# Layer 3's band matrices kept by pairs of outputs instead of tiles by outputs

## The chip, the cores and the metric

The kernel runs on one core of a Trainium2 chip. The metric is the device time of one execution in microseconds (us). Three runs of the kernel before gave 8943.62, 8946.06 and 8962.98 us; the median, 8946.06 us, is the time before. The profile is of a further execution, of 8976.86 us.

## The reference

A network of four layers works on x, 16 images of 64 x 64 pixels with 256 channels, in float32. Each layer is a residual block on the group-normalised input:

```
x = x + L0(gn(x))   # linear attention over the 4096 pixels, 8 heads
x = x + L1(gn(x))   # gated channels, a state-space scan over the pixels, batch norm
x = x + L2(gn(x))   # involution, 3 x 3 kernels made from the pixel itself
x = x + L3(gn(x))   # involution, 7 x 7 kernels made from the pixel itself
```

Only layer 3 is touched. It computes, with G = 16 groups of 16 channels:

```
r    = relu(bn(x @ w_reduce))                  # 256 -> 64
kgen = (r @ w_span + b_span).reshape(B, H, W, 16, 49)
out[b, h, w, g, c] = sum over the 49 taps k of kgen[b, h, w, g, k] * patch[b, h, w, k, g, c]
```

Every pixel has its own 49 weights for each group, and the 16 channels of a group share them.

## The kernel before

The layers run one after the other. Layer 3 is the last section of the program and takes the stretch from about 6608 us to the end.

**Tiles.** The image is cut into tiles of TR x TC = 3 x 8 output pixels: 22 rows of 8 tiles, so NTL = 176 tiles of TILE_OUT = 24 outputs. The input of a tile is 9 x 14 = 126 pixels (TILE_IN), which lie on the partitions. For a tile and a group, the 7 x 7 involution of the 24 outputs is one matrix product: a band matrix of 126 input pixels by 24 outputs, against the 126 pixels by the channels. The band matrix holds kgen at the 49 places of a column where the tap is, and zero elsewhere.

**The band matrices** are made by `matrices(i, quarter)` (L1362) for image i and a quarter of the channels, which is 4 groups. A quarter has two buffers `w` (tag "wm", pool of four buffers, so that of two quarters one is read while the other is made), one for each pair of groups: 128 partitions, and for each of them 176 tiles x 48 outputs (two groups of 24) of float32. Each buffer is made in 12 steps n of four output columns:

- TensorE (L1380): four float32 matmuls, each 64 rows (`span`, a shifted copy of the span weights) by 176 columns (`rt`, r for all 176 tiles at one output place). The profile records each float32 matmul as two instructions, each with its weight load. The results go to one of three PSUM tiles `pk` (tag "wg"), as [2, 2, 176]: b and m number the four outputs, and the last axis is the tile.
- The step's 4 x 176 numbers go from PSUM to `w` with the bias `spanb` added. In 14 of a quarter's 24 steps VectorE does it in one instruction of 704 elements (L1395); in the other 10 ScalarE does it in four of 176 elements (L1390). The innermost axis of each is the tile t, whose numbers are one after the other in PSUM and 48 floats (192 bytes) apart in `w`.

**The involution** is `involution7` (L1437), one turn for image i, a quarter, and t of NTT = 11. A turn has two rows of tiles (k = 0, 1), 8 tiles each, and two pairs of groups q: 32 float32 matmuls (L1446) of 126 rows, 32 output channels (`xw`, the patches, as weights) and 48 moving columns, the tile's slice of `w[q]`, 48 floats in a row. The four matmuls of one tj have their results on four different quarters of the partitions of the PSUM tile `pa`. ScalarE (L1456) and VectorE (L1457) then combine the two groups of a pair with masks into `ex`, and GpSimd (L1464) adds the residual `rx`.

**Order.** The loop at L1488 has 704 turns (16 images x 4 quarters x 11). A turn issues on SyncE's queue the patches of four turns ahead (L1414), the residual (L1434), the stores of finished outputs (L1526) and now and then the next image's features (L1314). Then come `involution7`, and `STEPS[t]` (3, 2, 2, 3, ...) steps of `matrices` for the quarter that is to come, so that 24 steps fit into 11 turns, and in many turns `reduced` (L1347 and L1354), which makes `rt` of the next image. The first quarter's matrices are made before the loop. In this section the order of the text is not binding: the framework's planner orders each engine's instructions by the place in the text and by when it reckons that operands and buffers are free, and places the semaphores. The order is fixed when the kernel is built.

`reduced` (L1347) has matmuls whose moving operand is read in pairs of floats, every second pair of a row (`"p (x b v) -> p b x v"`, b = 2, v = 2): the first pass of the chip over a layout like that of the change.

Of the kernel before, what the change touches and what calls it, by code (L numbers as in the profile page):

```python
# [9 lines left out]
F32 = mybir.dt.float32  # L10
# [5 lines left out]
P = 128  # L16
# [12 lines left out]
TR, TC = 3, 8  # L29
NTR, NTC = 22, HW // TC  # L30
TILE_IN = (TR + 6) * (TC + 6)
TILE_OUT = TR * TC
# [4 lines left out]
def network(ctx: ExitStack, tc: tile.TileContext, a: dict, out: bass.AP):  # L37
# [139 lines left out]
    with ExitStack() as st:  # L177
# [399 lines left out]
        for n in range(LAST + 16):  # L577
            m, t = divmod(n, NCH)
# [64 lines left out]
    with ExitStack() as st:  # L643
# [24 lines left out]
        with tc.tile_pool(name="s_conv", bufs=1) as pcv:  # L668
# [8 lines left out]
            for dj in range(7):  # L677
                dst = band if dj == 0 else term
# [22 lines left out]
        for n in range(10):  # L701
            delta, c = n // 2, n % 2
# [3 lines left out]
                rhs=maps[:, c, :, delta : delta + NB],  # L706
# [5 lines left out]
        m = maps[:, 0, :, 2 : 2 + NB]  # L712
# [18 lines left out]
        with tc.manual_schedule():  # L731
# [25 lines left out]
            for n, (ch, g) in enumerate(steps):  # L757
# [18 lines left out]
                b, k = g * 8, min(8, NI - g * 8)  # L776
# [8 lines left out]
        n = NI * NCH  # L785
# [500 lines left out]
    with ExitStack() as st:  # L1286
        pc = st.enter_context(tc.tile_pool(name="c_const", bufs=1))
        wk = st.enter_context(tc.tile_pool(name="c_work", bufs=2))
        wm_p = st.enter_context(tc.tile_pool(name="c_wm", bufs=4))
# [70 lines left out]
        NTL = NTR * NTC  # L1360

        def matrices(i, quarter):  # L1362


            rto = rts[i % 2].rearrange("k a b t u -> k (a b) (t u)")
            wms[i, quarter] = wm = []
            for q in range(2):
                w = wm_p.tile([P, NTL, 2 * TILE_OUT], F32, tag="wm", name="wm")
                wm.append(w)
                first = quarter * 4 + q * 2  # L1370
                for n in range(12):

                    pk = wg.tile([P, 2, CT], F32, tag="wg", name="pk")
                    pkv = pk[:, :, 0 : 2 * NTL].rearrange("p b (m t) -> p b m t", m=2)
                    for m in range(2):
                        for b in range(2):
                            gg, o = divmod(n * 4 + b * 2 + m, TILE_OUT)
                            s0 = SPAN - P - (o // TC * (TC + 6) + o % TC)
                            half = slice(b * 64, b * 64 + 64)
                            nc.tensor.matmul(  # L1380
                                pkv[:, b, m],
                                lhsT=span[half, first + gg, s0 : s0 + P],
                                rhs=rto[half, o // 4 * 2 + m, :],
                                start=True, stop=True,
                            )
                    g0 = first * TILE_OUT + n * 4
                    dst = w[:, :, n * 4 : n * 4 + 4].rearrange("p t (b m) -> p b m t", b=2)
                    if (q * 12 + n) % 12 in (1, 3, 6, 8, 11):
                        for m in range(4):
                            nc.scalar.activation(  # L1390
                                dst[:, m // 2, m % 2], pkv[:, m // 2, m % 2], AF.Identity,
                                bias=spanb[:, g0 + m : g0 + m + 1],
                            )
                    else:
                        nc.vector.tensor_tensor(  # L1395
                            dst, pkv,
                            spanb[:, g0 : g0 + 4].rearrange("p (b m) -> p b m", b=2).unsqueeze(
                                3
                            ).broadcast_to([P, 2, 2, NTL]),
                            ALU.add,  # L1400
                        )
                    yield
# [3 lines left out]
        NTT = NTR // 2  # L1406
# [30 lines left out]
        def involution7(i, quarter, t, wm, msk, xw, ex, rx):  # L1437


            pa = sm.tile([P, CT], F32, tag="sm", name="pa")  # L1440
            pav = pa[:, 0 : 2 * TR * HW].rearrange("c (g a w) -> c (g a) w", g=2, w=HW)
            for tj in range(NTC):
                for k in range(2):
                    for q in range(2):
                        p0 = 64 * k + 32 * q
                        nc.tensor.matmul(  # L1446
                            pav[p0 : p0 + 32, :, tj * TC : (tj + 1) * TC],
                            lhsT=xw[0:TILE_IN, k, tj, 32 * q : 32 * q + 32],
                            rhs=wm[q][0:TILE_IN, (t + k * NTT) * NTC + tj, :].rearrange(
                                "p (g w) -> p g w", w=TC  # L1450
                            ),
                            start=True, stop=True,
                        )
            pag = pa[:, 0 : 2 * TR * HW].rearrange("c (g t) -> c g t", g=2)
            h, pr = divmod(quarter, 2)
            nc.scalar.activation(ex, pag[:, 0], AF.Identity, scale=msk[:, pr, h, 0:1])  # L1456
            nc.vector.scalar_tensor_tensor(  # L1457
                ex, pag[:, 1], msk[:, pr, h, 1:2], ex, ALU.mult, ALU.add
            )
            parts = [(slice(0, P), TR * HW)]  # L1460
            if t == NTT - 1:
                parts = [(slice(0, 64), TR * HW), (slice(64, P), HW)]
            for p, m in parts:
                nc.gpsimd.tensor_tensor(ex[p, 0:m], ex[p, 0:m], rx[p, 0:m], ALU.add)  # L1464
# [19 lines left out]
        for _ in matrices(0, 0):  # L1484
            pass
        done = []
        gap = min(44, (4 * NTT * (NI - 1) - 4) // NCH)
        for n, (i, quarter, t) in enumerate(turns):  # L1488
# [17 lines left out]
            if t == 0:  # L1506
                making = iter(())
                if n + NTT < len(turns):
                    making = matrices(*turns[n + NTT][:2])
# [17 lines left out]
            if n + 2 in features:  # L1527
                cs[features[n + 2]] = load_reduced(*features[n + 2])
            involution7(i, quarter, t, wms[i, quarter], msk, pats.pop(0), ex[:, t % 2], rx[:, t % 2])
            if n % gap == 2 and n // gap < NCH:  # L1530
                strip_stores.extend(centred_strips(NI - 1, n // gap, xc, mean))
            for _ in range(STEPS[t]):
                next(making, None)
            if n in features:
                tp, k = features[n]
# [118 lines left out]
```

## Time and profile before

| | |
|---|---|
| Time before, median of three runs | 8946.06 us |
| Profiled execution: time, span | 8976.86 us, 8974.9 us |
| Layer 3, 6608 to 8975 us | 2367.00 us |
| in it: busy TensorE, VectorE, ScalarE, GpSimd | 1982.23, 1424.39, 1378.20, 455.48 us |
| in it: granted TensorE clock, share of the DMA engines, rate | 0.96, 0.80, 246 GB/s |
| L1395, VectorE, 704 elements, x896 | 1354 ns each |
| L1390, ScalarE, 176 elements, x2560 | 543 ns each |

The profile gives for each engine the time in which it was busy; TensorE has two rows, PE for the matmuls and PEld for the weight loads that run beside them. A group of instructions is named by its line in the program, its engine and "out<-in"; after x stands how many there were. "Idle before" is how long the engine had nothing to do ahead of them, and after "<-" what ended it. "issue" is time in which an engine waited for nothing that the profile shows. Instructions are recorded from start to end, so that neighbouring matmuls overlap.

### The profile page before, as it was taken

How to read it: one execution, taken by the hardware profiler on the slowest of the kernel's cores; microseconds unless marked ns; L12 is line 12 of the kernel's file. 1: busy time of each engine (PE TensorE's matmuls, PEld its weight loads, DVE VectorE, ACT ScalarE, POOL GpSimd, SP SyncE). 2: the span in 40 equal slices, each digit the busy share in tenths (PEclk: the TensorE clock that was granted, in tenths of full speed). 3: DMA queues.
4: the chain of work that ended last, by engine and by line, in shares of the span. 5: the costliest groups of instructions: out<-in, count | busy, mean ns of one | idle time of the engine just before them, and what ended most of it. 6: DMA issues, size and time to landing. Idle time of an engine off the chain costs nothing. (4 is left out here: it accounts for less than half of the span.)

```text
span 8974.9 us, 210876 instructions
## 1 busy us (share of the span) xinstructions
PE 7219.9 (80%) x84764; PEld 5328.9 (59%) x84764; DVE 6420.8 (72%) x8639; ACT 4992.0 (56%) x11904; POOL 2764.1 (31%) x1962
## 2 busy tenths in 40 slices
PE   7998988888899977477777777777758888888887
PEld 4666666666666653145554445545547666677776
DVE  6676666776666665679989988999946565566665
ACT  3555555555555554666655556565545555566655
POOL 0111111111111110157766666676712121111112
PEclk9999999999999987789888888888879999999999
DMA  6533333333333333867878878887768888888887
GB/s 219 167 121 122 122 124 123 125 118 125 127 106 104 106 113 118 250 201 219 222 215 226 223 217 223 227 224 211 182 193 240 248 249 244 247 256 255 255 256 233
DMA packets 1617971, 1695.46 MB, mean 189 GB/s; under 512 B 855265, under 2 KB 1221170, under 8 KB 1615842
## 3 DMA queue, kind: packets, MB, share of 16 engines
q1 hardware_dynamic: 1616994, 1681.98, 62.5%
q8 instruction: 668, 10.94, 0.5%
q14 instruction: 309, 2.53, 0.1%
HBM read 1234.54 MB, written 469.76 MB: 190 GB/s over the span
## 5 line engine op out<-in xcount | busy, mean ns | idle before, releaser
L279 PE MATMUL pq<-wq,xn 128*128 128x384 f32 x4096 | 1476.1, 504 | 105.4 <-DVE va L295 55.3
L1121 DVE TENSOR_TENSOR pd<-xs,pw 128x1152 f32<-128x1152 f32 x1024 | 1305.6, 1349 | 13.3 <-ACT xs L1102 13.3
L1380 PE MATMUL pk<-rt,span 64*128 64x176 f32 x12288 | 1217.4, 334 | 108.5 <-issue 58.5
L1395 DVE TENSOR_TENSOR wm<-pk,spanb 128x704 f32<-128x704 f32 x896 | 1174.2, 1354 | 171.6 <-PE pk L1380 157.7
L1390 ACT ACTIVATE wm<-pk,spanb 128x176 f32<-128x176 f32 x2560 | 989.8, 543 | 542.0 <-PE pk L1380 519.5
L1380 PEld LDWEIGHTS pk<-rt,span 64*128 64x128 f32 x12288 | 997.5, 195 | 212.5 <-issue 82.9
L1136 POOL TENSOR_TENSOR pd<-pd 128x2048 f32<-128x2048 f32 (+2 forms) x384 | 1064.6, 2772 | 180.9 <-DVE pd L1121 160.8
L279 PEld LDWEIGHTS pq<-wq,xn 128*128 128x128 f32 x4096 | 763.7, 195 | 572.7 <-DVE va L295 88.5
L1464 POOL TENSOR_TENSOR ex<-ex,rx 128x192 f32<-128x192 f32 (+2 forms) x768 | 436.8, 570 | 1888.1 <-DVE ex L1457 1401.0
L1446 PE MATMUL pa<-wm,xw 126*32 126x48 f32 x45056 | 694.4, 211 | 260.9 <-issue 245.8
L1457 DVE SCALAR_TENSOR_TENSOR ex<-pa,msk,ex 128x192 f32<-128x192 f32 x704 | 292.3, 415 | 752.2 <-ACT ex L1456 718.6
L1446 PEld LDWEIGHTS pa<-wm,xw 126*32 126x32 f32 x45056 | 574.4, 112 | 426.9 <-issue 376.2
L1098 PEld LDWEIGHTS pt<-ident,pad 128*128 128x128 f32 x4608 | 535.7, 150 | 239.6 <-issue 104.4
L1073 PE MATMUL pr<-x2r,wrs 128*64 128x512 f32 x512 | 364.5, 853 | 374.3 <-DMA x2r<-x_d 368.5
L1102 ACT COPY xs<-pt 128x512 f32<-128x512 f32 x1152 | 591.6, 602 | 121.1 <-PE pt L1098 115.5
L448 POOL TENSOR_TENSOR rsy<-ss,mhalf 128x4 f32<-128x4 f32 x128 | 129.8, 1014 | 1709.4 <-DVE ss L446 1709.4
L1098 PE MATMUL pt<-ident,pad 128*128 128x128 f32 x4608 | 615.7, 290 | 48.4 <-ACT rt L1076 29.3
L1271 DVE TENSOR_REDUCE x<-pd 128x512 f32<-128x4608 f32 x128 | 633.7, 4951 | 1.9
L1052 PE MATMUL px<-x2p,wis 128*128 128x512 f32 x1024 | 531.7, 664 | 111.4 <-ACT c L1150 68.2
L436 PE MATMUL py<-wo,oT 128*128 128x256 f32 x2048 | 472.8, 383 | 28.6 <-DVE va L295 28.6
L1456 ACT ACTIVATE ex<-pa,msk 128x192 f32<-128x192 f32 x704 | 298.3, 424 | 347.1 <-PE pa L1446 211.5
L445 ACT ACTIVATE sq<-y 128x256 f32<-128x256 f32 x512 | 213.0, 416 | 422.6 <-DVE y L441 414.6
(238 smaller groups left out, 12722.0 us busy)
## 6 DMA issues: line engine op xcount, KB each, us to landing
xw<-strips SPq DMA_DIRECT2D x1408, 256.0 KB
xn<-in_x SPq DMA_DIRECT2D x256, 512.0 KB
x_d<-x SPq DMA_DIRECT2D x256, 512.0 KB
strips<-xc SPq DMA_DIRECT2D x1536, 56.0 KB
xin<-in_x SPq DMA_DIRECT2D x128, 512.0 KB
x<-in_x SPq DMA_DIRECT2D x128, 512.0 KB
xm<-x_d SPq DMA_DIRECT2D x128, 512.0 KB
x<-x_d SPq DMA_DIRECT2D x128, 512.0 KB
```

The lines of the kernel that those rows point to most:

```text
L279: nc.tensor.matmul(pq[:, dd, 0:384], lhsT=xn[:, h, tok], rhs=wq[:, h, hf * 384 : (hf + 1) * 384], start=(h == 0), stop=(h == 1),)
L436: nc.tensor.matmul(py[:, q, :], lhsT=oT[hf][:, q * P : (q + 1) * P], rhs=wo[:, hf, :], start=(hf == 0), stop=(hf == 1),)
L1052: nc.tensor.matmul(px, lhsT=w[:, h, fh * P : (fh + 1) * P], rhs=x2[:, h], start=(h == 0), stop=(h == 1),)
L1098: nc.tensor.transpose(pt[:, k, h * P : (h + 1) * P], lines[:, h, rc * 4 + e + k, 2 * j : 2 * j + P], ident,)
L1102: nc.scalar.copy(xs[:, e : e + 2, j, :], pt)
L1121: nc.vector.tensor_tensor(pd[:, r].rearrange("p (g f) k -> p g f k", f=16), run[:, oh * 9 * P : (oh + 1) * 9 * P].rearrange("p (g f k) -> ...
L1136: nc.gpsimd.tensor_tensor(pd[..., 0:n], pd[..., 0:n], pd[..., n : 2 * n], ALU.add)
L1271: nc.vector.tensor_reduce(x3[:, :, P:C], pd1, AX.X, ALU.add)
L1380: nc.tensor.matmul(pkv[:, b, m], lhsT=span[half, first + gg, s0 : s0 + P], rhs=rto[half, o // 4 * 2 + m, :], start=True, stop=True,)
L1390: nc.scalar.activation(dst[:, m // 2, m % 2], pkv[:, m // 2, m % 2], AF.Identity, bias=spanb[:, g0 + m : g0 + m + 1],)
L1395: nc.vector.tensor_tensor(dst, pkv, spanb[:, g0 : g0 + 4].rearrange("p (b m) -> p b m", b=2).unsqueeze(3).broadcast_to([P, 2, 2, NTL]), AL ...
L1446: nc.tensor.matmul(pav[p0 : p0 + 32, :, tj * TC : (tj + 1) * TC], lhsT=xw[0:TILE_IN, k, tj, 32 * q : 32 * q + 32], rhs=wm[q][0:TILE_IN, (t ...
```

## The change

The buffer `w` is turned: instead of (tile, output) it is kept as (pair of outputs, tile, output of the pair), 24 pairs x 176 tiles x 2. It has the same size, and as many instructions as before write and read it.

```
-                w = wm_p.tile([P, NTL, 2 * TILE_OUT], F32, tag="wm", name="wm")
+                w = wm_p.tile([P, TILE_OUT, NTL, 2], F32, tag="wm", name="wm")
...
-                    dst = w[:, :, n * 4 : n * 4 + 4].rearrange("p t (b m) -> p b m t", b=2)
+                    dst = w[:, n * 2 : n * 2 + 2].rearrange("p b t m -> p b m t")
...
                         nc.tensor.matmul(
-                            pav[p0 : p0 + 32, :, tj * TC : (tj + 1) * TC],
+                            pav[p0 : p0 + 32, :, tj * TC : (tj + 1) * TC].rearrange(
+                                "c g (w v) -> c g w v", v=2
+                            ),
                             lhsT=xw[0:TILE_IN, k, tj, 32 * q : 32 * q + 32],
-                            rhs=wm[q][0:TILE_IN, (t + k * NTT) * NTC + tj, :].rearrange(
-                                "p (g w) -> p g w", w=TC
+                            rhs=wm[q][0:TILE_IN, :, (t + k * NTT) * NTC + tj].rearrange(
+                                "p (g w) v -> p g w v", w=TC // 2
                             ),
                             start=True, stop=True,
                         )
```

What VectorE and ScalarE write (L1395, L1390) now has neighbouring tiles 2 floats (8 bytes) apart instead of 192 bytes. What TensorE reads as the moving operand (L1446) is now 24 pairs of floats, 352 floats (1408 bytes) from one pair to the next, instead of 48 floats in a row. What is read from PSUM, what is written there, and all transfers stay.

## The prediction

> **What bounds the kernel now.** I read first the busy times of the stretch that the change touches, layer 3 (columns: stretch, its length, busy time and instructions of PE, PEld, VectorE, ScalarE, GpSimd; granted clock, DMA share, GB/s):
>
> ```profile
> 6608.00:8975.00 2367.00, 1982.23 (x58852) 1665.72 (x58852) 1424.39 (x1660) 1378.20 (x3759) 455.48 (x776) 0.96 0.80 246
> ```
>
> TensorE is busy for 84% of it, VectorE and ScalarE, which the change relieves, for 60% and 58%. So their time counts only where TensorE waits for them. Next, the groups of the page:
>
> ```profile
> L1380 PE MATMUL pk<-rt,span 64*128 64x176 f32 x12288 | 1217.4, 334 | 108.5 <-issue 58.5
> L1395 DVE TENSOR_TENSOR wm<-pk,spanb 128x704 f32<-128x704 f32 x896 | 1174.2, 1354 | 171.6 <-PE pk L1380 157.7
> L1390 ACT ACTIVATE wm<-pk,spanb 128x176 f32<-128x176 f32 x2560 | 989.8, 543 | 542.0 <-PE pk L1380 519.5
> L1446 PE MATMUL pa<-wm,xw 126*32 126x48 f32 x45056 | 694.4, 211 | 260.9 <-issue 245.8
> ```
>
> The writers of `wm` mostly wait for TensorE, not the reverse. TensorE's own waits (weight loads, 6700 to 8900 us; columns: total, times, longest):
>
> ```profile
> PEld pa L1446 <- issue: 352.1, 658, 3.6
> PEld pk L1380 <- issue: 80.3, 85, 3.0
> PEld pk L1380 <- DVE wm L1395: 44.8, 65, 2.1
> PEld pk L1380 <- ACT wm L1390: 21.1, 47, 0.7
> ```
>
> Only the last two are what the change can shorten. The big one, "issue", is explained by the timeline of the weight loads:
>
> ```profile
> 7066.72 0.52 PEld L1446 LDWEIGHTS pa<-wm,xw 126*32 126x32 f32 x41 [0.20 <-DMA rx<-c_d]
> 7068.76 0.32 PEld L1446 LDWEIGHTS pa<-wm,xw 126*32 126x32 f32 x23 [1.52 <-issue]
> ...
> 7073.57 0.66 PEld L1446 LDWEIGHTS pa<-wm,xw 126*32 126x32 f32 x55 [0.63 <-issue]
> ...
> 7078.41 0.24 PEld L1446 LDWEIGHTS pa<-wm,xw 126*32 126x32 f32 x15 [1.52 <-issue]
> ```
>
> The pauses fall in the middle of a turn's 64 loads, where nothing new is needed, 128 loads (256 instructions) apart and 4.8 us apart. Counted over TensorE's records, all 163 pauses over 0.9 us without a wait sit at one place modulo 256. The DMA queue that carries instructions shows why:
>
> ```profile
> q8 instruction: 668, 10.94, 0.5%
> ```
>
> 10.94 MB in 668 packets is 16 KB each, 256 instructions of 64 bytes. In layer 3 these packets come 5.09 us apart on average. I cut the stage into such blocks: 224 of 439 end in a pause over 0.5 us, 318 us of pauses in all. TensorE's floor here is thus its instruction supply, in half of the blocks, and its own work and waits in the other half.
>
> [...] writing at 192 bytes, VectorE takes 1354 ns for 704 elements, while this row of 1024 contiguous elements, also from PSUM with a repeated second operand, takes 1225 (min/median/max):
>
> ```profile
> L441 DVE TENSOR_TENSOR y<-py,bout x128: 1208/1225/1230, 243.0 to 3327.7; 128x1024 f32<-128x1024 f32 x128
> ```
>
> [...]
>
> **The change part by part.**
>
> *VectorE's writes.* [...] Best: the contiguous price[...]. Worst: 1354[...]. I take 892: GpSimd's L999 writes 512 elements at 8 bytes in 1278 ns, and the line through its contiguous L1464 (192 elements, 592) and L892 (1024, 2356) gives 1271 at 512. VectorE is relieved of 896 x 0.462 = 414 us.
>
> *ScalarE's writes.* L1456 takes 421 ns (median) for 192 contiguous elements[...]. From 542: 2560 x 0.134 = 343 us less. Bounds 408 and 542 likewise.
>
> Neither sum is a gain in itself: TensorE is the engine at work meanwhile, and most of both becomes waiting for `pk`.
>
> *TensorE's waits for them.* Over the whole run, L1380's loads waited 52.7 us for L1395 and 27.4 for L1390, L1446's 1.6 and 4.6: 86 us, which includes the 24 steps before the first turn. A wait averages 0.67 us (52.7 in 79) behind VectorE and 0.46 (27.4 in 60) behind ScalarE; each VectorE step shortens by 0.46, often two stand in a row, and a ScalarE step of four by 4 x 0.134 = 0.54. I take 85% as gone: 73 us. Bounds: 0 and 86.
>
> *Where that time goes.* Fetching is late next. In my blocks, 77 of 81 us of these waits lie in blocks that do not end in a pause. For each block I took the longer of its own work less 85% of its waits and the time at which its successor's packet had landed (plus the 1.45 us that TensorE resumes after it). This leaves 82% of the saving: 73 becomes 60 us.
>
> *TensorE's reads.* [...] The rows before have such a stream in L1347, pairs 16 bytes apart, two column strips at once: median 332 ns for 192 columns. L1380 (309 at 176, contiguous) and L1446 (206 at 48) give 0.80 ns per column, so 322 at 192: 10 ns for 96 pairs, 2.5 ns for L1446's 24. Its four strips start a new set every 43 ns; I take 45. 45056/4 = 11264 sets x 2 = 23 us, 55% of them in blocks that pause anyway; the same reckoning leaves 10 us. A gain is excluded: L1446 already streams at the 0.80 ns per column of the wider L1380. The other end is not shown: four strips[...], at a step of 1408 bytes. If they got in each other's way fully, a set would take 86 ns.
>
> *Unchanged:* PSUM traffic, every DMA and SyncE's queue, number and size of buffers, GpSimd. No wait is added: a matmul of L1446 needs all 24 steps of its quarter in either layout, and they end a quarter earlier.
>
> *Sum:* -60 + 10 = -50 us of 8976.86, to 8927, or -0.56%. On the median of the runs, 8946.06 x 0.9944 = 8896 us. The profiled execution is 0.3% slower than that median, which is carried as a ratio.
>
> **Rivals.**
>
> *The supply takes it all.* If fetches slip later as TensorE hurries, every block becomes fetch-bound and nothing is left: about 8940. For it: half of the blocks are so now, and DMA is busy 0.80. Against it: the waits lie in the other blocks.
>
> *The writes don't get cheaper.* Then VectorE stays at 1354, the reads cost their 10 us: 8956, or 8946 with no read price. Against it, L999 and the 417 ns of VectorE's L406 (256 elements in runs of 16 bytes[...]).
>
> *TensorE's reads collide: slower.* Place: the moving operand of L1446. Price: the reckoning by blocks, with the waits' gain taken off, gives -12 us at 10 ns more per set, +11 at 15, +35 at 20, +87 at 30 and +172 at 43. It decides from 43 to about 56 ns per set; at 86 the time is 9118. For it: no stream before has four strips in pairs, or pairs this far apart. Against it: two strips in pairs cost 3% in L1347, and four contiguous streams show no conflict (40 ns of streaming in 43).
>
> *The planner orders otherwise.* The timeline has runs of 4 and 20 loads of L1380, where a step has 8: TensorE's order is not the text's. If its estimates see the layout, the order moves, by perhaps the size of the waits (86 us) halved, to either side: 8900 to 8990.
>
> **How the numbers follow.** A measurement of this kernel tells about 0.2% (18 us) from no change. Forecast, evictions cheaper and reads nearly free: 0.66, 8870 to 8920. The supply takes it: 0.09. Writes no cheaper: 0.05. Reads collide: 0.15, a tenth of them too mild to be seen. Order: 0.05, split. So faster 0.69, same 0.14, slower 0.17. The range of 8 in 10 goes from 8860 (all waits gone, nothing absorbed, reads free) to 8975 (reads at 60 to 65 ns per set); beyond it lie most collisions, about 0.12, and 0.05 below. The likeliest case's own range is 8870 to 8920.
>
> **What would show it.** L1395 at about 890 ns and L1390 near 410; TensorE's loads waiting under 20 us for the two instead of 86; L1446 at 206 to 212 ns; the pauses still 256 instructions apart, somewhat longer in sum. Wrong would be: L1395 above 1200 ns (write price), L1446 above 230 ns or its busy time well over 694 us (collision), "issue" grown by 60 us or more (supply), or other run lengths of L1380 and L1446 in the timeline (planner).

## The result and the profile after

| | before | after |
|---|---|---|
| median of 20 runs each, beside each other | 8948.55 us (8930.47 to 8962.98) | 8936.84 us (8922.95 to 8945.3) |
| ratio, 95% interval | | 0.9984 (0.9977 to 0.9991) |
| profiled execution: time, span | 8976.86, 8974.9 us | 8935.19, 8932.9 us |

The change saves 12 us, 0.16% (0.09 to 0.23%). The prediction had 50 us. The profiled execution of before was 28 us above the median of its runs. I therefore use a second profiled execution of the same kernel (8947.42 us, span 8945.5) as the base of all sums below.

In the changed kernel the lines behind L1446 have moved by two (L1456 is L1458, L1464 is L1466). The busy times of layer 3 after:

```profile
6608.00:8932.00 2324.00, 2002.42 (x58790) 1694.03 (x58788) 1058.11 (x1656) 1272.62 (x3750) 456.82 (x776) 0.97 0.81 250
```

VectorE has lost 366 us of work against the 1424.39 of before, ScalarE 106. Of all this the time shows 12. The groups of the page:

```profile
L1390 ACT ACTIVATE wm<-pk,spanb 128x176 f32<-128x176 f32 x2560 | 846.7, 425 | 540.0 <-PE pk L1380 518.9
...
L1395 DVE TENSOR_TENSOR wm<-pk,spanb 128x704 f32<-128x704 f32 x896 | 789.7, 888 | 228.3 <-PE pk L1380 216.2
...
L1446 PE MATMUL pa<-wm,xw 126*32 126x48 f32 x45056 | 744.1, 215 | 214.7 <-issue 200.1
```

L1395 fell from 1354 to 888 ns and L1390 from 543 to 425. L1446's busy time rose by 50 us. TensorE's own waits, 6700 to 8860 us (total, times, longest), first in the repeat of before:

```profile
PEld pa L1446 <- issue: 325.6, 637, 4.2
PEld pk L1380 <- issue: 73.2, 80, 2.9
PEld pk L1380 <- DVE wm L1395: 43.2, 66, 1.7
PEld pr L1347 <- issue: 23.6, 107, 0.9
PEld pr L1347 <- DMA c<-c_d: 23.6, 12, 5.8
PEld pk L1380 <- ACT wm L1390: 20.4, 48, 0.7
```

and the same view of after:

```profile
PEld pa L1446 <- issue: 303.3, 639, 3.5
PEld pk L1380 <- issue: 75.7, 81, 3.5
PEld pr L1347 <- DMA c<-c_d: 28.6, 16, 4.3
PEld pr L1347 <- issue: 24.0, 101, 1.7
PEld pk L1380 <- ACT wm L1390: 19.5, 53, 0.5
PEld pk L1380 <- DVE wm L1395: 15.6, 33, 1.2
```

The waits for VectorE's evictions shrank by 28 us here, those for ScalarE's hardly. The three rows of "issue" fell too, from 422 us to 403, and the wait for `c` grew by 5 only, yet little came out. The rows count a pause only from the end of one record to the start of the next, and the matmuls of L1446 became longer. A ledger that adds start-to-start times of TensorE's weight loads sees both. It covers all of layer 3 in one profiled execution per kernel (us; worked out from the records; layer 3 runs from the first load of L1380 to the end of the span). The two executions of the kernel before, 2367 and 2356, and two of the changed kernel, 2331 and 2330, show how well such a length repeats. The rows repeat less well: "issue" in the view above sums to 422 us in the repeat of before and to 452 in its first execution, and the wait for `c` to 23.6 and 9.0. The last row of the table is from the clock records: TensorE's granted clock is in them either full or half, in stretches of 3.41 us or a multiple of it.

| | before, repeated | after | cheap writes alone | pair reads alone | pairs near | half evictions |
|---|---|---|---|---|---|---|
| layer 3 | 2356 | 2331 | 2332 | 2359 | 2318 | 2330 |
| waits for L1395 and L1390 | 119 | 67 | 69 | 118 | 73 | 50 |
| pauses without a wait (block ends above all) | 429 | 405 | 446 | 399 | 427 | 473 |
| L1446 streaming, load to load | 479 | 524 | 484 | 527 | 506 | 485 |
| waits for the features `c` and patches `xw` | 34 | 38 | 48 | 45 | 38 | 35 |
| L1380's loads, load to load, without a wait | 845 | 843 | 842 | 818 | 830 | 850 |
| time at half the clock | 195 | 164 | 192 | 130 | 158 | 173 |

After against before: the waits fell by 52 us, the streaming of L1446 rose by 45, the pauses fell by 24, and layer 3 is 25 us shorter, of which the timed runs confirm 12 to 16. The experiments take this apart.

### The profile page after: what moved, and what is told of

The parts are those of the page before. It is cut to its first block, busy times and chain, and to the rows that moved or that the text cites. A ratio compares the mean times of both kernels' runs of the same rounds, so it can differ in the third digit from the quotient of the medians.

```text
span 8932.9 us, 210876 instructions
## 1 busy us (share of the span) xinstructions
PE 7240.9 (81%) x84764; PEld 5356.7 (60%) x84764; DVE 6056.1 (68%) x8639; ACT 4887.9 (55%) x11904; POOL 2765.1 (31%) x1962
## 5 line engine op out<-in xcount | busy, mean ns | idle before, releaser
L1380 PE MATMUL pk<-rt,span 64*128 64x176 f32 x12288 | 1192.5, 331 | 75.6 <-issue 54.3
L1390 ACT ACTIVATE wm<-pk,spanb 128x176 f32<-128x176 f32 x2560 | 846.7, 425 | 540.0 <-PE pk L1380 518.9
L1380 PEld LDWEIGHTS pk<-rt,span 64*128 64x128 f32 x12288 | 985.0, 193 | 170.7 <-issue 80.6
L1466 POOL TENSOR_TENSOR ex<-ex,rx 128x192 f32<-128x192 f32 (+2 forms) x768 | 438.0, 572 | 1842.5 <-DVE ex L1459 1335.7
L1395 DVE TENSOR_TENSOR wm<-pk,spanb 128x704 f32<-128x704 f32 x896 | 789.7, 888 | 228.3 <-PE pk L1380 216.2
L1446 PE MATMUL pa<-wm,xw 126*32 126x48 f32 x45056 | 744.1, 215 | 214.7 <-issue 200.1
L1446 PEld LDWEIGHTS pa<-wm,xw 126*32 126x32 f32 x45056 | 619.9, 112 | 380.7 <-issue 330.2
L1458 ACT ACTIVATE ex<-pa,msk 128x192 f32<-128x192 f32 x704 | 299.8, 426 | 393.5 <-PE pa L1446 230.7
```

The source lines that it names most:

```text
L1380: nc.tensor.matmul(pkv[:, b, m], lhsT=span[half, first + gg, s0 : s0 + P], rhs=rto[half, o // 4 * 2 + m, :], start=True, stop=True,)
L1390: nc.scalar.activation(dst[:, m // 2, m % 2], pkv[:, m // 2, m % 2], AF.Identity, bias=spanb[:, g0 + m : g0 + m + 1],)
L1395: nc.vector.tensor_tensor(dst, pkv, spanb[:, g0 : g0 + 4].rearrange("p (b m) -> p b m", b=2).unsqueeze(3).broadcast_to([P, 2, 2, NTL]), AL ...
L1446: nc.tensor.matmul(pav[p0 : p0 + 32, :, tj * TC : (tj + 1) * TC].rearrange("c g (w v) -> c g w v", v=2), lhsT=xw[0:TILE_IN, k, tj, 32 * q ...
```

## The experiments

**1. The two halves of the change, each alone.** The layout of the change with L1446 reading 48 floats in a row (other numbers than those it should read, so the output is not the reference's), and the old layout, written as before, with L1446 reading pairs 1408 bytes apart (not the reference's either):

```
cheap writes alone:
-  w = wm_p.tile([P, NTL, 2 * TILE_OUT], ...)
+  w = wm_p.tile([P, TILE_OUT, NTL, 2], ...)
-  dst = w[:, :, n * 4 : n * 4 + 4].rearrange("p t (b m) -> p b m t", b=2)
+  dst = w[:, n * 2 : n * 2 + 2].rearrange("p b t m -> p b m t")
+  rhs=wm[q].rearrange("p b t v -> p (b t v)")[0:TILE_IN, 48*j : 48*j + 48]...
pair reads alone:
+  rhs=wm[q].rearrange("p t o -> p (t o)").rearrange("p (b t v) -> p b t v", t=NTL, v=2)[0:TILE_IN, :, j]...
```

> The buffer is laid out and written as in the changed kernel (pairs, 8 bytes apart), but L1446 reads 48 floats in a row from it, as before, so the involution multiplies other numbers than it should. Theory (ledger): the changed kernel gained about 42 us of TensorE's waits for VectorE and lost about 46 us in slower sets of L1446, and the instruction supply swallows part of both. Then this run has L1395 at 891 ns, sets of four L1446 every 43 ns, waits for L1395 as short as in the changed kernel, and is about 35 us faster than before (0.996). Rival (the supply takes it all): about as the changed kernel, 0.998 to 1.000, with pauses between instruction blocks longer by what the waits lost.

> The buffer is laid out and written as before (192 bytes apart), but L1446 reads 24 pairs of floats 1408 bytes apart from it, as in the changed kernel, so the involution multiplies other numbers than it should. Theory (ledger): L1395 at 1354 ns, sets of four L1446 every 48 ns instead of 43, about 46 us more streaming, half of it swallowed by shorter pauses between instruction blocks: about 20 us slower than before (1.002 to 1.003). Rival (the reads cost only what the prediction put, 10 us, and the supply took the gain): 1.000 to 1.001.

Measured: cheap writes alone 8931.53 us beside 8945.47, ratio 0.9987 (0.998 to 0.9994). Pair reads alone 8947.35, ratio 0.9997 (0.9986 to 1.0008). So all of the gain comes from the writes, and it is small without any price of the reads. The waits with cheap writes alone:

```profile
PEld pa L1446 <- issue: 331.8, 638, 3.7
PEld pk L1380 <- issue: 75.6, 82, 3.5
PEld pr L1347 <- DMA c<-c_d: 34.5, 12, 5.4
PEld pr L1347 <- issue: 29.6, 108, 2.9
PEld pk L1380 <- ACT wm L1390: 19.6, 54, 0.5
PEld pk L1380 <- DVE wm L1395: 16.5, 34, 1.2
```

VectorE's row is at 16.5 instead of 43.2, but the three "issue" rows together are 437 us instead of 422 (L1347's was 23.6 in the repeat), and the wait for `c` is 34.5 instead of 23.6. In the ledger, 36 of the 50 us of waits saved come back: 17 as pauses, 14 as late transfers and 5 as streaming. Rows of this size differ as much between the two executions of the kernel before, so this one trace doesn't settle the split; that 50 us of waits brought 14 us of time is what the timed runs show.

The reads, on the other hand, cost 48 us of streaming that the time doesn't show. In the ledger the pauses are 30 us shorter. Another 27 us come from L1380's own loads, which no edit touched: in this execution TensorE ran at half the clock for 130 us of layer 3 instead of 195. Whether the shorter pauses raised the clock was not tried. L1446 in the run with the reads alone (min/median/max):

```profile
L1446 PE MATMUL pa<-wm,xw x45056: 202/211/291, 6622.0 to 8952.8; 126*32 126x48 f32 x200
```

The four matmuls of a set take 48 ns from set to set here (median; 46 to 52 in the middle half), against 43 (42 to 43) before. As I read it, a slower stream only brings TensorE to the end of its block later, where the next block is not there yet: the pauses are 399 us in this run, 429 in the repeat of before.

**2. Pairs, but near.** The layout of the change, with L1446 reading pairs 16 bytes apart (again not the right numbers):

```
+  rhs=wm[q]... [start : start + 96].rearrange("p (g w x v) -> p x g w v", x=2, v=2, w=TC // 2)[:, 0]
```

> As the first of these runs, but L1446 reads 24 pairs of floats 16 bytes apart (every second pair of 96 floats in a row), so the involution multiplies other numbers than it should. Theory A [...]: sets every 46 to 48 ns as in the changed kernel, time as the changed kernel (0.998). Theory B (the distance of 1408 bytes costs): sets every 43 to 44 ns, time as the first of these runs (0.996).

Measured: 8930.75 us, ratio 0.9984 (0.9976 to 0.9992), a set every 45 ns, and the matmul back at nearly its old length:

```profile
L1446 PE MATMUL pa<-wm,xw x45056: 202/207/291, 6612.1 to 8905.7; 126*32 126x48 f32 x200
```

So of the 5 ns that a set costs more, 2 are for the pair (what the prediction took from L1347) and 3 for the distance of 1408 bytes, which it had put at nothing. In the time neither shows.

**3. A third of the transfers left out.** The second tile row's patches are not loaded and the first row's are used for both (not the reference's output): 184 MB less over the span, and the DMA engines in layer 3 are busy 0.64 instead of 0.81. In this kernel the old layout, the cheap writes alone, and the whole change:

```
-  for k in range(2):           # loads of xw
+  for k in range(1):
-  lhsT=xw[0:TILE_IN, k, tj, 32 * q : 32 * q + 32]
+  lhsT=xw[0:TILE_IN, 0, tj, 32 * q : 32 * q + 32]
```

> The kernel before with half of its patches left out: the second tile row of a turn is not loaded, and the first row's patches are multiplied in its place. The work of TensorE, VectorE and ScalarE is the same, the transfers of layer 3 are about a third fewer. Supply theory (instruction blocks wait behind the transfers): the pauses at block ends fall from about 390 us to 200 or less, and the kernel is 150 us or more faster (0.98). Rival (the pauses don't come from busy transfer engines): pauses and time stay within 30 us of before.

> Half of the patches left out as in the kernel just named, the buffer written by pairs and read 48 floats in a row (other numbers multiplied). Supply theory: with the supply out of the way the 42 us of waits for VectorE that go come out in the time, 35 us or more below the light kernel with the layout of before, where the full kernel showed 12. Rival (the gain went elsewhere, not to the supply): again 10 to 15 us.

> Half of the patches left out, the layout of the changed kernel for writes and reads. Supply theory: the 46 us of slower sets of L1446 are no longer swallowed, so this one is 30 us or more slower than the light kernel with pair writes and contiguous reads, and about level with the light kernel with the layout of before. Rival: as fast as the light kernel with contiguous reads.

Measured, as ratios to the kernel before: 0.9769 (0.9753 to 0.9786), 0.9729 (0.9716 to 0.9742) and 0.9735 (0.9721 to 0.975); medians 8719.57, 8682.41 and 8687.91 us. Leaving out the transfers alone brings 204 us; in the ledger the pauses of the old layout fall from 429 to 263 us, and TensorE is at half the clock for 89 us of layer 3 instead of 195. With fewer transfers the cheap writes bring 37 us instead of 14. The reads cost 5.5 us more, within the uncertainty, where the theory wanted 30 or more: they are still covered. The ledger shows how (waits for evictions 101, 51, 50 us; pauses 263, 290, 239): the pauses have become fewer but are still there.

**4. The dose.** If a removed wait were worth 82% of itself, evictions of half the length should bring far more. Only 88 of the 176 tiles are copied, and L1446 reads the copied half alone (not the reference's output), with all transfers and with a third left out. The light kernel with the old layout was run again as the base of the latter.

```
-  dst, pkv, ...broadcast_to([P, 2, 2, NTL])
+  dst, pkv[:, :, :, 0 : NTL // 2], ...broadcast_to([P, 2, 2, NTL // 2])     # L1390 likewise
```

> The layout of the change with the reads kept contiguous, and every eviction of layer 3 only half as long (88 of the 176 tiles of each output are copied, and the matmuls of L1446 read the copied half alone; the output is not the reference's). VectorE's step falls to about 0.5 us, ScalarE's to 1.2 us or less, so nearly all of the 118 us of waits for evictions in the kernel before should be gone, where the run with the cheaper writes took 50 of them. Theory of the prediction (82% of a removed wait comes out): the time falls by 70 to 95 us against the kernel before. Theory that the supply of instructions and the late transfers take it: the pauses between blocks and the waits for c grow, and the time falls by 35 us or less.

> The kernel before without the load of the second tile row's patches (the first row's are used twice; the output is not the reference's), as the base of the next run: 0.975 to 0.979 of the kernel before by its first run.

> Evictions of half length (as two runs above) in the kernel that doesn't load the second tile row's patches (the output is not the reference's in either respect). With fewer transfers beside it the supply should take less back: if so, the time falls by 60 us or more against the light kernel with the old layout, well over what the half evictions bring with all transfers. If the supply is not the reason, both give the same, within 15 us.

Measured: 8932.34 us beside 8944.06, ratio 0.9985 (0.9978 to 0.9993). That is what the cheap writes gave, and no more. The groups and the waits of this run:

```profile
L1390 ACT ACTIVATE wm<-pk,spanb 128x88 f32<-128x88 f32 x2560 | 652.7, 343 | 592.8 <-PE pk L1380 569.1
...
L1395 DVE TENSOR_TENSOR wm<-pk,spanb 128x352 f32<-128x352 f32 x896 | 466.0, 522 | 381.2 <-PE pk L1380 364.4
```

```profile
PEld pa L1446 <- issue: 343.6, 665, 3.8
PEld pk L1380 <- issue: 81.8, 85, 3.3
PEld pr L1347 <- issue: 46.2, 109, 4.4
...
PEld pa L1446 <- DVE wm L1395: 14.0, 47, 0.9
...
PEld pk L1380 <- ACT wm L1390: 8.4, 36, 1.7
PEld pk L1380 <- DVE wm L1395: 5.8, 7, 0.9
```

The waits of L1380 for both engines are 14 us instead of 64, though L1446 now waits 14 us for VectorE, and "issue" has grown in every row: 472 us in all, against 422 in the repeat of before. Cut into blocks of 256 instructions, 249 of 449 now end in a pause over 0.5 us, 336 us of pauses in all. The repeat of before had 215 of 443 and 298 us, its first execution 224 of 439 and 318, so the pauses grew by 18 to 38 us. In the pausing blocks TensorE still goes on 1.4 us (median) after its packet has landed. This fits the rival "the supply takes it"; the light pair below shows it more clearly.

The half evictions have two side effects on TensorE. Its queue has 544 more instructions that only handle semaphores, of 51 ns each, and 796 of its 58852 loads stand at another place in the order. The added instructions cost nothing where they stand: L1380's first load after L1446 starts 175 ns (median) after the load before it, with such an instruction between as without. But they are two blocks more to fetch, at 5.00 us from block to block an estimate of 10 us at most.

The light pair: 8737.46 and 8711.07 us, ratios 0.9769 and 0.974 (0.9725 to 0.9754), a gain of 26 us. I had expected 60 or more if the supply took less back; by the words of that expectation, 26 against 12 counts as the same. Its premise, that lighter transfers free the supply, was wrong. The waits of the light kernel with half evictions:

```profile
PEld pa L1446 <- issue: 262.6, 616, 3.5
PEld pk L1380 <- issue: 66.3, 86, 2.3
...
PEld pk L1380 <- DVE wm L1395: 6.9, 8, 1.2
PEld pk L1380 <- ACT wm L1390: 5.8, 31, 0.2
```

and of its base:

```profile
PEld pa L1446 <- issue: 263.1, 661, 3.9
PEld pk L1380 <- issue: 37.7, 56, 2.3
PEld pk L1380 <- DVE wm L1395: 29.5, 41, 1.6
```

Here L1380's "issue" grew by 29 us as its waits went (L1446's wait for VectorE grew too, from 8 us to 21). Counted over all of layer 3, 173 blocks end in a pause, with 220 us of pauses; in the two runs of the base it was 145 and 130 blocks, with 175 and 162 us. That is well over what these two differ by. Fewer transfers do not end the limit, they lower it: a block that ends in a pause takes 4.45 us (mean) with the light transfers and 4.78 with all. The clock is not the reason, since blocks that ran at the full clock throughout show the same, 4.42 and 4.74. That the light kernels keep more of a removed wait (37 and 26 us against 14 and 12) fits, but with four runs each of the light ones the intervals are wide.

**5. ScalarE's share.** The waits for L1390 hardly moved, so I gave ScalarE fewer of the 24 steps on the changed layout: 6 (twice) and 4 instead of 10. VectorE takes the others. The changed kernel was run again beside the one with 4.

```
-  if (q * 12 + n) % 12 in (1, 3, 6, 8, 11):
+  if (q * 12 + n) % 12 in (1, 5, 9):      # six; four: (3, 9)
```

> The changed kernel with 6 instead of 10 of a quarter's 24 steps on ScalarE (n = 1, 5, 9 of each 12), 18 on VectorE. ScalarE's step of four takes 1.32 us in the changed kernel, VectorE's 0.89. If TensorE's remaining 40 us of waits for L1390 matter, they fall below 20 and the kernel is 15 us or more faster than the changed one (0.9965 of before). If the supply takes what waits give back, the waits fall too but the time stays at 0.998 to 0.999.

> The changed kernel itself, beside the three below: the base that they are compared with. By its own earlier result 10 to 15 us faster than the kernel before (ratio 0.998), with about 30 us of waits of L1347 for the features c in layer 3, 40 us of waits for ScalarE's copies and 28 us for VectorE's.

> The changed kernel with ScalarE's evictions cut further, to steps 3 and 9 of each 12 (4 of 24 steps in place of 10; the run with 6 of 24 came 31 us under the kernel before). If the wait for ScalarE's step of 1.32 us is what is left to gain: waits for ScalarE below 20 us and as fast as with 6 steps or a few us faster. If VectorE becomes the bound: 20 steps of 0.89 us make 17.8 us of each 24 steps, waits for VectorE above 60 us and the time at or above the changed kernel's.

> The changed kernel with ScalarE's evictions at steps 1, 5 and 9 of each 12, once more. If its first result holds: 25 to 35 us under the kernel before. In that run's trace layer 3 began 30 us earlier than elsewhere and was itself only 12 us shorter than in the changed kernel; if that was the execution and not the edit: 10 to 20 us under the kernel before, like the changed kernel itself.

Measured: changed again 8934.75 us beside 8950.74, ratio 0.9981 (0.9974 to 0.9989). Four steps: 8935.62, 0.9984 (0.9977 to 0.999). Six steps: 8892.22 beside 8923.31, 0.9967 (0.9955 to 0.9979), and the second time 8921.09 beside 8944.06, 0.9976 (0.9967 to 0.9986). The first run of six steps looks like 31 us. But in its trace layer 3 begins at 6563.5 us, where all others have 6582 to 6608, ahead of anything that the edit touches; its layer 3 is only 12 us shorter than that of the changed kernel. The second gives 23 us, with a layer 3 that is 2 us shorter. Six steps are thus faster than the kernel before, and by the ratios perhaps 4 to 13 us faster than the changed one; the intervals of the two overlap. The waits don't explain such a gain: L1380's for ScalarE are 15.1 and 16.6 us in the two traces, against 19.3 in the changed kernel run again, but L1446's for VectorE are 17.5 and 19.0, against 7.6. With four steps the waits move to VectorE further: L1380 waits 6.2 us for ScalarE and 25.6 for VectorE, L1446 18.1 for VectorE.

**6. The features earlier.** The wait for `c` (24 to 37 us in the ledger) looked like time for the taking. Its load was issued one turn earlier, in the changed kernel and in the one with six ScalarE steps:

```
-  if n + 2 in features:
-      cs[features[n + 2]] = load_reduced(*features[n + 2])
+  if n + 3 in features:
+      cs[features[n + 3]] = load_reduced(*features[n + 3])
```

> The changed kernel with one edit more: the load of the features c of layer 3 is issued one turn (of the loop over groups) earlier. Theory that the saved time was lost to late transfers: the 30 us of waits for c fall below 10 us, and 10 to 20 us come out in the time against the changed kernel run beside it. Rival, that the supply of instructions takes whatever is saved in this layer: the waits for c fall, the pauses between blocks of instructions grow by as much, and the time stays within 5 us of the changed kernel. Third: c is waited for as long as before, because its load is held up by its queue and not by its place; no change in waits or time.

> The changed kernel with both edits: ScalarE's evictions at steps 1, 5 and 9 of each 12 and the features loaded one turn earlier. If the two gains are of different waits and not taken back: the sum of the two, 30 to 45 us under the kernel before. If the supply takes what is saved: no more than with the fewer ScalarE steps alone (about 20 us under the changed kernel).

Measured: 8936.31 us, ratio 0.9989 (0.9981 to 0.9997), and 8935.81, 0.9984 (0.9977 to 0.9991). Neither is faster than the changed kernel beside them (8934.75). In the ledger the wait for `c` fell from 24 to 8 us in the first. The pauses did not grow there, as the rival had it (408 to 396 us), but the waits for VectorE went from 31 to 45 and layer 3 was no shorter (2335 us against 2330). So it is not only the supply of instructions that takes a saving back; what exactly moved in this run stays open. No version that was run is shown to beat the changed kernel beyond its uncertainty.

## Why the prediction was wrong

*VectorE's writes: right.* 892 ns forecast, an estimate of mine; 888 measured against 1354 before, and 888 with cheap writes alone. Two rows of before bear the estimate: a straight line through 417 ns for 256 elements (L406, runs of 16 bytes) and 1225 for 1024 in a row (L441) gives 888 at 704. What makes the writes at 192 bytes cost more was not shown.

*ScalarE's writes: the duration nearly right, the step not.* A single activation fell to 425 ns (408 forecast, an estimate of mine below the 421 ns that L1456 took for 192 elements). But the four of a step overlap. The step in the timeline of ScalarE, before:

```profile
7070.07 1.55 ACT L1390 ACTIVATE wm<-pk,spanb 128x176 f32<-128x176 f32 x4 [0.32 <-PE pk L1380]
```

and after:

```profile
7070.91 1.31 ACT L1390 ACTIVATE wm<-pk,spanb 128x176 f32<-128x176 f32 x4 [0.39 <-PE pk L1380]
```

By the medians, the four started 363, 319 and 319 ns apart and now start 310, 292 and 290 apart, so the step went from 1.545 to 1.322 us. It shortened by 0.22 us, not by the 4 x 0.134 = 0.54 of the prediction. Neighbouring activations of a step overlap by about 224 ns in the trace of before (543 less 319) and by 133 in that of after (425 less 292). This term was mis-sized, and the waits for ScalarE fit it: they only fell from 49 to 40 us in the ledger.

*TensorE's waits: 73 of 86 us gone forecast, 35 of 87 measured by the same count.* The forecast added what the loads of L1380 and L1446 waited over the whole run. The repeat of before has 87 us of it. After, the views of L1395 and then of L1390, under "who waited for it", give 53:

```profile
  PEld pk L1380: 19.3, 38
...
  PEld pa L1446: 5.7, 24
...
  PEld pk L1380: 24.6, 66
...
  PEld pa L1446: 3.0, 12
```

VectorE's part fell from 54 to 25 us and ScalarE's from 33 to 28. The ledger, which counts from start to start, has more to begin with, and 52 of 119 us gone (VectorE's 70 to 28, ScalarE's 49 to 40). By either count the "85% as gone" was about twice too large, and ScalarE's part fell shortest of it.

*What of it is kept: the step that failed.* "This leaves 82% of the saving." Measured with cheap writes alone, 50 us of waits in the ledger (35 by the smaller count) became 14 us of time, and with half evictions 69 us (54) became 12. Even the layer's own length in single profiled executions, 24 and 25 us shorter, is half of the ledger's waits at most. The last 19 us of waits taken away brought nothing that the runs show.

The reckoning by blocks took the time at which each packet had landed, counted from the start of its block, as fixed: where a block did not pause, the packet that was there early gave room. That the waits lay in blocks that don't pause was right (72 of 77 us in the repeat), and so was the warning beside it, "if fetches slip later as TensorE hurries". The runs with half evictions show that pauses grow as waits go: 249 pausing blocks and 336 us, against 224 and 318 or 215 and 298 in the two executions of before, and in the light kernel 220 us against 175 or 162. For the change's own size of saving, the growth of 17 us is no more than those two executions differ by. This case had been given 0.09.

The explanation that fits is that a block can't go through much faster than its packets come, so that a wait inside it is mostly time that TensorE would have spent on the next packet anyway. It is not one fixed time: pausing blocks take 4.78 us in the mean, but half of them lie outside 4.35 to 5.21. The direct test, a kernel that does the same work with fewer instructions for TensorE, was not run. So the step that failed is shown, and what took the saving is shown in part.

*The reads: mis-sized, and cheaper than forecast all the same.* A set takes 48 ns, not 45. The gross price is 45 to 48 us instead of 23, and the net one about 0 instead of 10. The argument for the net price, that a slow block eats its own pause, was right and stronger than reckoned: between cheap writes alone and the whole change the pauses fall by 41 us, as much as the streaming grows by. In the run with the reads alone part of it was luck, since 27 us came from L1380's loads in an execution with half the clock for 130 us instead of 195, which the argument did not have.

*The rivals.* "The supply takes it all" gave 8940 and came nearest. It is not quite all: 12 to 16 us are left. "Writes no cheaper" falls with 888 ns. "Reads collide" falls: 48 ns is under the 56 at which it would have decided. "The planner orders otherwise" falls: all 58852 loads of layer 3 stand in the same order in both kernels. Of the signs named beforehand, "issue grown by 60 us or more" for the supply appeared in no run. The three rows sum to 403 us after, where the longer reads shorten them, to 437 with cheap writes alone and to 472 with half evictions, against 422 before: 49 us at most. A sign for one mechanism should be read with the other edits of the change taken off. "Under 20 us" for the waits was missed as well, with 53.

Two slips in the working carry no weight: 48 columns at 0.80 ns are 38 ns of streaming per set, not 40, and a matmul of L1446 needs the 12 steps of its own buffer `w`, not all 24 of its quarter.

## What to carry to other kernels

When an engine pauses at regular counts of instructions, as TensorE did here every 256, suspect its instruction supply as a floor under many stretches of its work, and don't price the waits between the pauses as free time to be had. Here taking away 50 of 119 us of them returned 14 us, and taking away 69 returned 12. The same pauses can hide small losses: 45 us of slower reads showed no cost in the time. Before pricing a removed wait, ask what the engine would reach sooner, and price a run of overlapping instructions by start to start, not by duration: ScalarE's four activations of 425 ns took 1.32 us together.

## What the runs showed of the hardware

- A set of four 48-column float32 strips of L1446 took 45 ns with the moving operand in pairs of floats 16 bytes apart (pairs near) and 48 at 1408 bytes (pair reads alone), against 43 with 48 floats in a row (before).
- VectorE's eviction of 704 elements took 1354 ns at 192 bytes from element to element and 888 at 8; ScalarE's of 176 elements 543 and 425, with starts 319 and 291 ns apart inside a step.
- TensorE's packets of 256 instructions come 5.07 us apart in layer 3 of the repeat of before, and 5.00 with half evictions. A block that ends in a pause took 4.78 us (mean) with the DMA engines busy 0.81, and 4.45 with 0.64. 215 of 443 blocks in the repeat of before end in a pause over 0.5 us, 298 us in all. What sets the 4.8 us, besides the transfers, was not tried.
- TensorE's clock in layer 3 was half for 195 us in the repeat of before, 164 in the changed kernel, 130 with pair reads alone and 87 to 89 in the light kernel with the old layout. L1380's loads without a wait took 845, 843, 818 and 819 us there.
- In one profiled execution of six ScalarE steps layer 3 began at 6563.5 us, in the other of the same program at 6582, and in all other runs at 6588 to 6608. No edit touched what lies before it, and the reason is open.
